# A graph layer on one core: six edges in a partition instead of eight, 36-node spans about each group's middle edge, a written instruction order

## The chip, the core and the metric

The kernel runs on one core of a Trainium2 chip. The metric is device time in microseconds (us) of one execution, as the median of several runs; lower is better. A profile is one more execution, recorded by the hardware profiler.

## The reference

12,500 nodes have 128 features each (`x`), and 412,500 edges have 48 (`edge_attr_48`). `dst` gives each edge's node and is sorted, so a node's edges lie together: 33 of them on average, one of which is the node's own loop.

```python
h = jnp.maximum(_layernorm(x, axis=-1), 0.0)
agg = jax.ops.segment_sum(edge_attr_48, dst, num_segments=12500)
u = graph_globals[zeros(12500)]          # one graph
t = jnp.concatenate([h, agg, u], axis=1) # 128 + 48 + 64
out = x + jax.nn.relu(t @ W1 + b1) @ W2 + b2   # 240 -> 256 -> 128
```

All numbers are 32-bit floats.

## The kernel before

**Sums over edges.** A chunk is 1024 edges (`CE`), laid out as 128 partitions with 8 edges each (`T`); there are 403 chunks, the last one partly filled. Four chunks (`CG`) make a group, and there are 101 groups (`NG`). `group` (L186) loads a group's edges (768 KB, `load_edges`, L170), builds one-hot rows on VectorE (L194: 32 edge slots times 48 nodes, `W`, equal or not equal to the edge's place in its chunk's span), and lets TensorE multiply edges by one-hots (L201: 32 matmuls with 48 moving columns, put by turns into PSUM rows 0 to 47 and 64 to 111). `add` (L212) reads the group's first node into a register of VectorE (L207) and adds the group's PSUM tile, 141 nodes wide, into `aggT` at that node (L214). `aggT` holds the sums of all nodes, transposed.

**The spans and their check.** The place of an edge is its node less the base of its chunk, and the base (`brow`, L141) is the node of the group's first edge, less 8, plus 31 for each chunk. `read_dst` (L242) reads `dst` for 128 chunks with one chunk in a partition, subtracts the bases (L249), transposes the result into `rel`, and takes each chunk's least and greatest place (L251, L252). The last chunk has too few edges, so `load_dst` (L220) fills its row with the last edges of `dst` once more (L229); a filled slot has zero features, so it changes no sum. L267 to L281 fold the extremes into one flag: `bad` (L279) becomes 1 if any place lies outside 0 to 47, or if the groups' first nodes run too far from an even pace. Every engine loads the flag into a register (L280), and if it is 1, the block from L284 to L333 runs.

**The block behind the flag.** It serves any input: it clears `aggT`, finds each chunk's least and greatest node, and then loops over the chunks at run time (L325), one chunk in a round. A round loads the chunk's edges into a single buffer, reads the two nodes into registers (L308), and runs an inner loop over windows of 64 nodes (L313): one-hots, eight matmuls, and one addition into `aggT`. At the end it sets `rel` so that the groups that follow add nothing. In the profile no line between L285 and L333 appears.

**The MLP.** Nodes go in 25 blocks: one of 212 and 24 of 512. `normalize` (L364) takes mean and variance on VectorE and scale and shift on ScalarE. `mlp` (L382) adds `b2` to `x` on GpSimd (L386), normalizes on ScalarE (L390), transposes on TensorE (L392), copies to SBUF on ScalarE (L395), multiplies by `W1` (L399 for `h`, L400 for the sums), applies relu on ScalarE (L402), multiplies by `W2` (L407), adds on VectorE (L409) and stores. A block may start when the groups that hold its nodes have been added (`ready`, L91).

**Order.** A scheduler of the language places the instructions on each engine; the program states only the order of the calls (L420 to L438). Edge loads and stores go through SP's DMA queue, `x` and the weights through ScalarE's.

Of the kernel before, what the change touches and what calls it, by code (L numbers as in the profile page):

```python
# [9 lines left out]
F32 = mybir.dt.float32  # L10
# [11 lines left out]
def kernel(  # L22
# [24 lines left out]

    nc = tc.nc
# [4 lines left out]
    T = 8  # L53
    CE = P * T
    CG = 4
    GE = CG * CE
    STEP = N * CE // E
    SL = 8
    W = 48
    WG = STEP * (CG - 1) + W  # L60
# [12 lines left out]
    EARLY = 6  # L73
    MARGIN = 64
    GSTEP = CG * STEP
# [13 lines left out]
    supers += [rest[i:i + XB] for i in range(0, len(rest), XB)]  # L89

    ready = [min(NG - 1, -(-(a + R * m + MARGIN) // GSTEP) - 1) for a, m in blocks]  # L91

    const = ctx.enter_context(tc.tile_pool(name="const", bufs=1))
    big = ctx.enter_context(tc.tile_pool(name="big", bufs=1))
    psum = ctx.enter_context(tc.tile_pool(name="ps_agg", bufs=1, space=bass.MemoryType.PSUM))

    rel = big.tile([P, NB * P, T], F32)
    aggT = big.tile([P, N + SL + WG], F32)
    brow = const.tile([1, NB * P], F32)
    lo_i = const.tile([1, NG], I32)  # L100
    span = const.tile([P, NB, 2], F32)
    bad = const.tile([1, 1], I32)

    first = const.tile([1, NG], I32)
    with nc.allow_non_contiguous_dma(reason="a hundred numbers, once"):
        nf = E // GE
        nc.sync.dma_start(first[:, :nf], dst[:nf * GE].rearrange("(a g e) -> a g e", a=1, e=GE)[:, :, 0])
        if nf < NG:
            nc.sync.dma_start(first[:, nf:NG], dst[None, nf * GE:nf * GE + 1])

    one = const.tile([1, 1], F32)
    nc.gpsimd.memset(one, 1.0)
    steps = const.tile([1, NG, CG], F32)
    nc.gpsimd.iota(steps, pattern=[[0, NG], [STEP, CG]], base=-SL, channel_multiplier=0,
                   allow_small_or_imprecise_dtypes=True)
    least = const.tile([1, NG], F32)
    nc.gpsimd.iota(least, pattern=[[GSTEP, NG]], base=-MARGIN, channel_multiplier=0,
                   allow_small_or_imprecise_dtypes=True)
    ident = const.tile([P, P], F32)
    make_identity(nc, ident)  # L120
    iota = const.tile([P, WA], F32)
    nc.gpsimd.iota(iota, pattern=[[1, WA]], base=0, channel_multiplier=0,
                   allow_small_or_imprecise_dtypes=True)
    eps = const.tile([P, 1], F32)
    nc.gpsimd.memset(eps, EPS)
    nc.gpsimd.memset(aggT, 0.0)
    nc.gpsimd.memset(span, 0.0)
    warm = const.tile([P, 1], F32)
    nc.scalar.activation(warm, eps, AF.Sqrt, bias=eps)

    acc = []
    for i in range(3):
        ps = psum.tile([P, 512], F32, name=f"ps{i}")
        nc.vector.memset(ps, 0.0)
        acc.append(ps)


    lo_f = const.tile([1, NG], F32)
    nc.vector.tensor_scalar(lo_f, first, 0.0, float(N - 1), OP.max, OP.min)
    nc.vector.tensor_copy(lo_i, lo_f)  # L140
    nc.vector.tensor_tensor(brow[:, :NG * CG].rearrange("a (g k) -> a g k", k=CG), steps,  # L141
                            lo_f[:, :, None].to_broadcast([1, NG, CG]), OP.add)


    w1h = const.tile([D, H], F32)
    w1a = const.tile([P, H], F32)
    w1u = const.tile([G, H], F32)
    w2 = const.tile([P, NH, D], F32)
    b1_sb = const.tile([P, NH], F32)
    u = const.tile([G, 1], F32)  # L150
    b2_sb = const.tile([P, D], F32)
    bias = const.tile([P, NH], F32)
    nc.gpsimd.memset(w1a, 0.0)

    def load_weights():
        nc.scalar.dma_start(w1h, W1[0:D])
        nc.scalar.dma_start(w1a[0:DE], W1[D:D + DE])
        nc.scalar.dma_start(w1a[HI:K2], W1[D:D + DE])
        nc.scalar.dma_start(w1u, W1[D + DE:D + DE + G])
        nc.scalar.dma_start(w2, W2.rearrange("(a p) d -> p a d", p=P))  # L160
        with nc.allow_non_contiguous_dma(reason="a few hundred numbers, once"):
            nc.scalar.dma_start(b1_sb, b1.rearrange("(a p) -> p a", p=P))
            nc.scalar.dma_start(u, graph_globals[0:1].rearrange("a g -> g a"))
        nc.scalar.dma_start(b2_sb, b2[None, :].to_broadcast([P, D]))

    ep = ctx.enter_context(tc.tile_pool(name="edges", bufs=8))
    ohp = ctx.enter_context(tc.tile_pool(name="oh", bufs=3))
# [18 lines left out]
    def group(g):  # L186
        c0 = g * CG
        n = min(CG, NCH - c0)
        wg = STEP * (n - 1) + W
        e = ep.tile([P, CG, T * DE], F32, name="e")  # L190
        load_edges(e, c0, n)
        oh = ohp.tile([P, CG * T, W], F32, name="oh")
        r = rel[:, c0:c0 + n, :].rearrange("p c t -> p (c t)")
        nc.vector.tensor_tensor(  # L194
            oh[:, :n * T], iota[:, None, :W].to_broadcast([P, n * T, W]),
            r[:, :, None].to_broadcast([P, n * T, W]), OP.is_equal)
        ps = acc[g % len(acc)]
        for k in range(n):
            for t in range(T):
                h = HI * (t % 2)  # L200
                nc.tensor.matmul(  # L201
                    ps[h:h + DE, STEP * k:STEP * k + W], e[:, k, t * DE:(t + 1) * DE], oh[:, k * T + t, :],
                    start=(k == 0 and t < 2), stop=(k == n - 1 and t >= T - 2), skip_group_check=True)
        return ps, wg

    def first_node(g):
        _, at = nc.values_load_multi_w_load_instructions(  # L207
            lo_i[0:1, g:g + 1], engines=[DVE], min_val=0, max_val=N - 1,
            skip_runtime_bounds_check_because="clamped to 0..N-1 on the chip")
        return at[0]  # L210

    def add(g, ps, wg):  # L212
        at = first_node(g)
        nc.vector.tensor_tensor(aggT[:K2, ds(at, wg)], aggT[:K2, ds(at, wg)], ps[:K2, :wg], OP.add)  # L214


    with tc.tile_pool(name="dst", bufs=2) as dp, tc.tile_pool(
        name="ps_dst", bufs=2, space=bass.MemoryType.PSUM
    ) as ps_dst:
        def load_dst(b):  # L220
            rows = min(P, NCH - b * P)
            full = min(P, NFULL - b * P)
            di = dp.tile([P, CE], I32, name="di")
            if full:
                nc.sync.dma_start(
                    di[:full], dst[b * P * CE:(b * P + full) * CE].rearrange("(c e) -> c e", e=CE))
            if full < rows:
                nc.sync.dma_start(di[full:rows, :TAIL], dst[None, E - TAIL:E])
                nc.sync.dma_start(di[full:rows, TAIL:], dst[None, E - (CE - TAIL):E])  # L229
            return di, rows  # L230

        def spread(b, df, rows):
            dv = df.rearrange("c (p t) -> c t p", t=T)
            for t0 in range(0, T, 4):
                pt = ps_dst.tile([P, 4, P], F32, name="ptd")
                for t in range(4):
                    nc.tensor.transpose(pt[:, t, :rows], dv[:rows, t0 + t, :], ident[:rows, :rows])
                nc.scalar.copy(  # L238
                    rel[:, b * P:b * P + rows, t0:t0 + 4].rearrange("p c t -> p t c"),
                    pt[:, :, :rows])  # L240

        def read_dst(b):  # L242
            di, rows = load_dst(b)
            df = dp.tile([P, CE], F32, name="df")
            pb = ps_dst.tile([P, 1], F32, name="pb", bufs=1)
            nc.tensor.matmul(pb[:rows], brow[:, b * P:b * P + rows], one, start=True, stop=True)  # L246
            base = dp.tile([P, 1], F32, name="base")
            nc.vector.tensor_copy(base[:rows], pb[:rows])
            nc.vector.tensor_scalar(df[:rows], di[:rows], base[:rows], None, OP.subtract)  # L249
            spread(b, df, rows)  # L250
            nc.vector.tensor_reduce(span[:rows, b, 0:1], df[:rows], AX.X, OP.min)  # L251
            nc.vector.tensor_reduce(span[:rows, b, 1:2], df[:rows], AX.X, OP.max)  # L252

        read_dst(0)
        load_weights()
        waiting = []
        for g in range(EARLY):
            waiting.append((g, *group(g)))
            if len(waiting) > 1:
                add(*waiting.pop(0))  # L260
            if g + 1 < NB:
                read_dst(g + 1)
        for w in waiting:
            add(*w)


        worst = const.tile([P, NB, 2], F32)  # L267
        nc.vector.tensor_scalar(worst[:, :, 0], span[:, :, 0], -1.0, None, OP.mult)
        nc.vector.tensor_scalar(worst[:, :, 1], span[:, :, 1], float(1 - W), None, OP.add)
        wcol = const.tile([P, 1], F32)  # L270
# [163 lines left out]
    for w in waiting:  # L434
        add(*w)
# [31 lines left out]
```

## Time and profile before

| | |
|---|---|
| median of 3 runs | 418.35 us (418.1 to 421.17) |
| the profiled execution, its own time | 418.65 us |
| its span, first to last instruction | 416.9 us |
| TensorE matmuls, busy | 342.9 us, 82% of the span |
| VectorE busy | 283.7 us, 68% |
| ScalarE, GpSimd busy | 106.4 us, 81.0 us |
| moved by DMA | 95.20 MB, 228 GB/s on average |
| first edge matmul starts at | 23.2 us |

The profiled execution took 0.3 us more than the median. Of its 418.65 us, 1.75 us lie outside the span. In the profile's rows PE is TensorE, PEld its weight loads, DVE VectorE, ACT ScalarE, POOL GpSimd and SP the engine that issues DMAs; a q behind the name means the engine's sequencer. A 32-bit matmul stands in the trace as two records. L201 is line 201 of the kernel.

### The profile page before, as it was taken

The page shows a single profiled execution, that of the slowest core. Times are in us where ns is not written, and L with a number is a line of the kernel's source. Part 1 is how long each engine was busy: PE and PEld are TensorE (multiplying, and loading weights), DVE is VectorE, ACT ScalarE, POOL GpSimd, SP SyncE. Part 2 cuts the span into 40 slices and gives each one's busy share as a digit, 9 for nine tenths or more (in the row PEclk, how much of TensorE's full clock was granted, in tenths as well). Part 3 has the DMA queues.
Part 4 walks back from the last instruction along what each step waited for, and adds up shares of the span by engine and source line. Part 5 has one row for each costly group of instructions (what it writes and reads, how often), then busy time and mean ns, then how long its engine had stood idle before and what let it go on. Part 6 is the DMA issues. An engine that isn't in the chain of part 4 may idle for free.

```text
span 416.9 us, 15948 instructions
## 1 busy us (share of the span) xinstructions
PE 342.9 (82%) x7193; PEld 270.0 (65%) x7194; DVE 283.7 (68%) x472; ACT 106.4 (26%) x193; POOL 81.0 (19%) x41
## 2 busy tenths in 40 slices
PE   0487569998699989898986997995979998888985
PEld 0377555785477677577565777774768776757853
DVE  7898598764965696786377788467675668629510
ACT  1140027312213303331230330330321332131231
POOL 9300021120221120222022022112022112203200
PEclk9995689999999999999899999999889999989999
DMA  5997693559847978877596697696583898654000
GB/s 163 323 370 264 207 346 126 188 197 308 286 141 239 323 255 304 281 248 233 179 322 217 225 316 233 192 342 219 198 302 109 257 325 270 194 198 156 29 13 39
DMA packets 61720, 95.20 MB, mean 228 GB/s; under 512 B 2760, under 2 KB 54996, under 8 KB 61649
## 3 DMA queue, kind: packets, MB, share of 16 engines
q1 hardware_dynamic: 57287, 87.26, 62.4%
q10 hardware_dynamic: 4362, 6.89, 4.7%
q8 instruction: 57, 0.93, 0.9%
q14 instruction: 14, 0.11, 0.1%
HBM read 87.74 MB, written 6.40 MB: 226 GB/s over the span
## 4 chain that ended last, share of the span: by engine, by line
PE 40%; issue 17%; DMA 10%; DVE 10%; POOL 5%; ACT 3%; DVEq 1%; ACTq 0%; POOLq 0%
PE ps L201 17%; DMA xt<-in_x_dram 10%; PE po L407 8%; PE ph L399 7%; PE ph L400 6%; POOL xb L386 5%; DVE oh L194 4%; DVE st L372 3%; ACT hT L395 3%; PE pt L392 2%; DVE mv L373 1%; DVE ot L409 1%; DVE aggT L214 1%; DVEq L207 1%; ACT hid L402 0%
## 5 line engine op out<-in xcount | busy, mean ns | idle before, releaser
L201 PE MATMUL ps<-oh,e 128*48 128x48 f32 x6448 | 175.8, 214 | 39.4 <-issue 17.7
L201 PEld LDWEIGHTS ps<-oh,e 128*48 128x48 f32 x6448 | 163.2, 130 | 53.8 <-DVE oh L194 21.9
L194 DVE TENSOR_TENSOR oh<-iota,rel 128x1536 f32<-128x1536 f32 (+1 forms) x101 | 194.0, 1936 | 2.3 <-ACT rel L238 1.3
L386 POOL TENSOR_TENSOR xb<-xt,b_sb 128x512 f32<-128x512 f32 (+1 forms) x25 | 67.7, 2709 | 313.6 <-DVE ot L409 273.6
L395 ACT COPY hT<-pt 128x512 f32<-128x512 f32 (+1 forms) x25 | 26.9, 1076 | 186.3 <-PE pt L392 186.3
L399 PE MATMUL ph<-hT,w1h 128*128 128x512 f32 (+1 forms) x100 | 56.4, 647 | 8.0 <-ACT hT L395 7.9
L214 DVE TENSOR_TENSOR aggT<-aggT,ps 112x141 f32 (+1 forms) x101 | 29.6, 293 | 47.8 <-PE ph L400 44.0
L407 PEld LDWEIGHTS po<-w,hid 128*128 128x128 f32 (+1 forms) x400 | 49.9, 189 | 16.5 <-issue 10.4
L407 PE MATMUL po<-w,hid 128*128 128x128 f32 (+1 forms) x400 | 55.4, 281 | 1.2 <-ACT hid L402 1.1
L409 DVE TENSOR_TENSOR ot<-po,xb 128x512 f32<-128x512 f32 (+1 forms) x25 | 17.2, 688 | 51.3 <-PE po L407 49.0
L400 PE MATMUL ph<-aggT,w1a 112*128 112x512 f32 (+1 forms) x100 | 52.0, 602 | 0.0
L402 ACT ACTIVATE hid<-ph,bias 128x512 f32<-128x512 f32 (+1 forms) x50 | 33.6, 676 | 47.5 <-PE ph L400 47.5
L390 ACT ACTIVATE xn<-xt,sh,sc 128x128 f32<-128x128 f32 (+1 forms) x100 | 40.7, 484 | 3.7 <-DVE sh L378 3.7
L372 DVE BATCH_NORM_STATS2 st<-xt 128x6 f32<-128x128 f32 (+1 forms) x100 | 25.1, 262 | 22.0 <-DMA xt<-in_x_dram 22.0
L400 PEld LDWEIGHTS ph<-aggT,w1a 112*128 112x128 f32 x100 | 20.3, 203 | 24.6 <-issue 24.0
L399 PEld LDWEIGHTS ph<-hT,w1h 128*128 128x128 f32 x100 | 18.3, 204 | 23.0 <-ACT hT L395 10.3
L392 PE MATMUL pt<-ident,xn 128*128 128x128 f32 (+1 forms) x100 | 18.1, 296 | 1.6 <-ACT xn L390 1.2
L373 DVE BATCH_NORM_AGGREGATE mv<-st 128x2 f32<-128x6 f32 (+1 forms) x100 | 15.6, 162 | 0.0
L246 PE MATMUL pb<-one,brow 1*128 1x1 f32 (+1 forms) x8 | 2.0, 312 | 14.6 <-DVE brow L141 13.8
L392 PEld LDWEIGHTS pt<-ident,xn 128*128 128x128 f32 (+1 forms) x100 | 11.1, 144 | 3.8 <-POOL xb L386 1.3
L376 ACT ACTIVATE sc<-mv,eps 128x16 f32<-128x16 f32 (+1 forms) x7 | 2.1, 305 | 42.0 <-DVE mv L373 42.0
L238 ACT COPY rel<-ptd 128x512 f32<-128x512 f32 (+1 forms) x8 | 6.7, 910 | 20.7 <-DMA w1a<-in_L_gnn_W_dram 13.4
(46 smaller groups left out, 59.9 us busy)
## 6 DMA issues: line engine op xcount, KB each, us to landing
e<-in_edge_attr_dram SPq DMA_DIRECT2D x100, 768.0 KB, 7.5
xt<-in_x_dram ACTq DMA_DIRECT2D x6, 1024.0 KB
out_dram<-ot SPq DMA_DIRECT2D x24, 256.0 KB, 5.3
di<-in_dst_dram SPq DMA_DIRECT2D x3, 512.0 KB, 11.1
e<-in_edge_attr_dram SPq DMA_DIRECT2D x1, 384.0 KB, 6.5
e<-in_edge_attr_dram SPq DMA_DIRECT2D x1, 159.0 KB
w1h<-in_L_gnn_W_dram ACTq DMA_DIRECT2D x1, 128.0 KB
w<-in_L_gnn_W_dram ACTq DMA_DIRECT2D x1, 128.0 KB, 4.2
```

The lines of the kernel that those rows point to most:

```text
L194: nc.vector.tensor_tensor(oh[:, :n * T], iota[:, None, :W].to_broadcast([P, n * T, W]), r[:, :, None].to_broadcast([P, n * T, W]), OP.is_e ...
L201: nc.tensor.matmul(ps[h:h + DE, STEP * k:STEP * k + W], e[:, k, t * DE:(t + 1) * DE], oh[:, k * T + t, :], start=(k == 0 and t < 2), stop= ...
L214: nc.vector.tensor_tensor(aggT[:K2, ds(at, wg)], aggT[:K2, ds(at, wg)], ps[:K2, :wg], OP.add)
L372: nc.vector.bn_stats(st[:m, i * R + r, :], xs[j][:m, r, :])
L386: nc.gpsimd.tensor_tensor(xb[:m], xs[j][:m], b2_sb[:m, None, :].to_broadcast([m, R, D]), OP.add)
L390: nc.scalar.activation(xn[:m, r], xs[j][:m, r], AF.Relu, bias=shift[j][:m, r:r + 1], scale=scale[j][:m, r:r + 1])
L392: nc.tensor.transpose(pt[:, r, :m], xn[:m, r], ident[:m, :m])
L395: nc.scalar.copy(hT[:, :n].rearrange("d (p r) -> d r p", r=R), pt[:, :, :m])
L399: nc.tensor.matmul(ph[:, :n], w1h[:, a * P:(a + 1) * P], hT[:, :n], start=True, stop=False)
L400: nc.tensor.matmul(ph[:, :n], w1a[:K2, a * P:(a + 1) * P], aggT[:K2, SL + a0:SL + a0 + n], start=False, stop=True)
L402: nc.scalar.activation(hid[:, a, :, :m], ph[:, :n].rearrange("h (p r) -> h r p", r=R), AF.Relu, bias=bias[:, a:a + 1])
L407: nc.tensor.matmul(po[:m, r], hid[:, a, r, :m], w2[:, a], start=(a == 0), stop=(a == NH - 1))
```

## The change

- A chunk is 768 edges, six in a partition; there are 538 chunks, and the last one holds 84 edges. Six chunks make a group (4608 edges, 36 one-hot slots, 864 KB), and there are 90 groups.
- A span is 36 nodes. The base of a chunk counts from the node of the group's middle edge (`mids`) with steps of 23 or 24 nodes (`OFF` is -76, -53, -29, -6, 17, 41). Places are now measured from the middle of the span, `MID` = 17.5, so that one reduction of the absolute value per 128 chunks replaces the two of before (`check_dst`), and the flag becomes 1 if the greatest absolute value is above 17.5 (`decide`).
- The row of the last chunk is filled as before: `load_dst` is the same text with the new sizes, so the fill is 684 edges.
- The block behind the flag stays, as the function `any_order`; its loop has 537 rounds and one more for the last chunk.
- `aggT` is cleared by ScalarE in five pieces (`clear`) and no longer by GpSimd (L126). The first eight groups' edges are issued at the start, and each later one behind a group's matmuls. `x` plus `b2` moves from GpSimd to VectorE. The variance comes from the halves that the statistics instruction gives, for 16 rows at once, in place of L373.
- `tc.manual_schedule()` makes each engine's order that of the calls. The MLP is cut into pieces (two `hidden`, one `transpose` of the next block, one `output`), which are dealt out between groups by a running budget; `store` follows one group later.

```diff
-    T = 8
+    T = 6
-    CG = 4
+    CG = 6
-    STEP = N * CE // E
-    SL = 8
-    W = 48
+    SL = 6
+    W = 36
+    MID = (W - 1) / 2
+    OFF = [round(N * CE / E * (k - CG / 2)) - SL for k in range(CG)]
...
+    ctx.enter_context(tc.manual_schedule())
...
-        nc.sync.dma_start(first[:, :nf], dst[:nf * GE].rearrange("(a g e) -> a g e", a=1, e=GE)[:, :, 0])
+    mids = [min(g * GE + GE // 2, E - 1) for g in range(NG)]
+        nc.sync.dma_start(first[:, :h], dst[:h * GE].rearrange("(a g e) -> a g e", a=1, e=GE)[:, :, GE // 2])
...
+    for k in range(CG):
+        nc.gpsimd.memset(steps[:, :, k], OFF[k] + MID)
...
+    nc.vector.tensor_scalar(iota, iota, -MID, None, OP.add)
...
-            nc.vector.tensor_reduce(span[:rows, b, 0:1], df[:rows], AX.X, OP.min)
-            nc.vector.tensor_reduce(span[:rows, b, 1:2], df[:rows], AX.X, OP.max)
+    def check_dst(b, df, rows):
+        nc.vector.tensor_reduce(span[:rows, b:b + 1], df[:rows], AX.X, OP.max, apply_absolute_value=True)
...
+    def decide():
+        wcol = const.tile([P, 1], F32)
+        nc.vector.tensor_reduce(wcol, span, AX.X, OP.max)
...
+        nc.vector.tensor_scalar(wrow[:, :P], pw, -MID, None, OP.add)
+        nc.vector.tensor_scalar(least, least, GSTEP, float(LEAST), OP.mult, OP.add)
+        nc.vector.tensor_tensor(wrow[:, P:], least, lo_f, OP.subtract)
+        wmax = const.tile([1, 1], F32)
+        nc.vector.tensor_reduce(wmax, wrow, AX.X, OP.max)
+        nc.vector.tensor_scalar(bad, wmax, 0.0, 1.0, OP.max, OP.min)
...
+    onehot(0)
+    for g in range(EARLY):
...
+        onehot(g + 1)
+        contract(g)
+        load_group(g + PF)
+        if g:
+            add(g - 1)
...
+    isbad = nc.values_load(bad[0:1, 0:1], min_val=0, max_val=1,
+                           skip_runtime_bounds_check_because="clamped to 0..1 on the chip")
+    any_order(isbad, hots[EARLY])
...
+    for g in range(EARLY, NG + LAG):
+        if g < NG:
+            onehot(g + 1)
+            contract(g)
+            load_group(g + PF)
+        if EARLY <= g - 1 < NG:
+            add(g - 1)
+        for j in late:
+            store(j)
...
+        while nextp < len(pieces) and done < budget and (pieces[nextp][1] <= g or g >= NG):
+            cost, _, run = pieces[nextp]
+            run()
```

`onehot`, `contract` and `add` hold what `group` and `add` held. The functions of the fill and of the block, as they stand in the changed kernel:

```python
    def load_dst(b):
        rows = min(P, NCH - b * P)
        full = min(P, NFULL - b * P)
        di = dp.tile([P, CE], I32, name="di", bufs=3)
...
        if full < rows:
            nc.sync.dma_start(di[full:rows, :TAIL], dst[None, E - TAIL:E])
            nc.sync.dma_start(di[full:rows, TAIL:], dst[None, E - (CE - TAIL):E])
...
                with tc.For_i(0, NFULL, 1) as c:
                    e = ap.tile([P, T * DE], F32, name="e2")
                    nc.sync.dma_start(e, edge_attr[ds(c * CE, CE)].rearrange("(p t) d -> p (t d)", t=T))
                    windows(e, rel[:, ds(c, 1), :].rearrange("p c t -> p (c t)"), ds(c, 1))
```

`windows` is the inner loop of before (L307 to L323) with six matmuls in place of eight.

## The prediction

> **What bounds the kernel now.** I read the engines' shares on the page first, then the page's groups, then the busy time of the edge matmuls in three stretches of the steady stage.
>
> ```profile
> PE 342.9 (82%) x7193; PEld 270.0 (65%) x7194; DVE 283.7 (68%) x472; ACT 106.4 (26%) x193; POOL 81.0 (19%) x41
> ```
>
> ```profile
> L201 PE MATMUL ps<-oh,e 128*48 128x48 f32 x6448 | 175.8, 214 | 39.4 <-issue 17.7
> L399 PE MATMUL ph<-hT,w1h 128*128 128x512 f32 (+1 forms) x100 | 56.4, 647 | 8.0 <-ACT hT L395 7.9
> L407 PE MATMUL po<-w,hid 128*128 128x128 f32 (+1 forms) x400 | 55.4, 281 | 1.2 <-ACT hid L402 1.1
> L400 PE MATMUL ph<-aggT,w1a 112*128 112x512 f32 (+1 forms) x100 | 52.0, 602 | 0.0
> ```
>
> ```profile
> 318.00:322.80 4.80, 4.80 (x210) 4.74 (x210) 1.00 0.56 151
> ```
>
> TensorE is the bound. Where it has work, 210 records of edge matmuls take 4.80 us (the columns are PE and PEld busy, with counts): 22.9 ns each, without a gap. From 318 to 400 us it is busy for 74.5 of 82 us. VectorE's largest group, the one-hots (101 times 1936 ns), runs beside it. So by its shares this is a kernel that could gain from narrower spans and fewer waits. What decides here, though, is a place of the profile that is nearly empty: the passage of the flag. These are the answers for the tile `bad` and for the branch at L284 (duration min/median/max in ns, then the first and last start in us), and then what followed in order of time (start and duration in us).
>
> ```profile
> L279 DVE TENSOR_SCALAR bad<-wmax x1: 142/142/142, 43.9 to 43.9; 1x1 int32<-1x1 f32 x1
> L280 PEldq TENSOR_LOAD <-bad x1: 488/488/488, 44.1 to 44.1; - x1
> ```
>
> ```profile
> L284 SPq EVENT_SEMAPHORE  x9: 17/17/17, 45.2 to 48.2; - x9
> ...
> L284 PEldq COMPARE_BRANCH  x1: 444/444/444, 44.7 to 44.7; - x1
> ```
>
> ```profile
> 45.71 0.52 PEld L344 LDWEIGHTS po<-u,w1u 64*128 64x128 f32 x4 [2.75 <-PEq L284]
> ...
> 48.34 0.32 ACTq L358 DMA_DIRECT2D xt<-in_x_dram  x1
> ```
>
> The flag is written at 44.09 us, every engine loads it and branches, and the next work is line 344, behind the block. The block was not entered. To pass it cost TensorE 1.6 us (45.71 - 44.09) and ScalarE 4.25 us (48.34 - 44.09).
>
> **Part 1: which way the flag falls.** The flag depends on `dst` alone, so it can be worked out by hand. The last chunk (537) is chunk 3 of group 89. That group's middle edge is 89 x 4608 + 2304 = 412,416, only 84 edges before the end; its node is 12,497. The middle of the chunk's span is 12,497 + OFF[3] + MID = 12,497 - 6 + 17.5 = 12,508.5. The chunk has 84 edges of its own, and its row in the check is filled with the last 684 edges of `dst`. At 33 edges to a node these reach back 20.7 nodes: to node 12,479. The place of that one is 12,479 - 12,508.5 = -29.5, and the limit is 17.5. So `decide` sees 29.5 - 17.5 = 12, clamps it to 1, and the flag is up. All other chunks lie within 15.5; the real edges of the last one do as well. A filled slot adds nothing to the sums, but the check counts it. Before, the fill was 172 edges, about five nodes, and all places lay from 4 to 46 in a span of 0 to 47; so the trace passed by. I therefore forecast that the changed kernel enters `any_order` on these inputs: the sums of the first groups are thrown away, all chunks are summed in a loop at run time, `rel` is overwritten, and the main loop then runs in full on one-hots that match nothing.
>
> **Part 2: one round of the loop.** No row of before shows it, so it is put together, with ends for each piece.
> - The edges' load. 144 KB go into a single buffer, and SP lets nobody into the inner loop until all its transfers are in. The issue of an edge load is 0.37 us in the timeline. The nearest rows for the landing:
>
> ```profile
> w1u<-in_L_gnn_W_dram ACTq DMA_DIRECT2D x1, 64.0 KB, 2.3
> w<-in_L_gnn_W_dram ACTq DMA_DIRECT2D x1, 128.0 KB, 4.2
> ```
>
>   Both stem from a start with full queues, and in the loop nothing else moves. I take 2.6 + 0.4 = 3.0 us (ends 2.3 and 4.6). The two register loads (0.3 to 0.5 us each) lie under it.
> - Three meetings of all five engines: into the inner loop, back out of it, and back to the next round. Each is drains, semaphores and a branch. The nearest row is the passage above: 1.6 us as TensorE saw it, of which 0.5 was the register's load, but that was one wait, and a loop's back edge has to reset semaphores between two of them. I take 1.5 us each, 4.5 in a round. [...] Ends: 0.7 us (the rows of single branches and semaphores are 17 to 444 ns) and 3.2.
> - The work between. Shift of the places 0.17 us; one-hot of 384 elements, from 1.72 us for 1536: 0.43, with a fixed part 0.5; twelve records of 64 columns, from 22.9 ns at 48: 12 x 30 ns = 0.37, with their latency 0.6; the addition 0.3, as L214; hand-overs 0.3. Together 1.9 us (1.3 to 2.2). A chunk's span is below 64 nodes, so the inner loop runs once.
>
> A round: 3.0 + 4.5 + 1.9 = 9.4 us (5.7 to 16.4). There are 537 rounds and the last chunk's: 538 x 9.4 = 5057 us. Nothing hides it: `add` on VectorE, the next groups' matmuls, the prefetched edges and the loads of `x` all stand behind the block on their engines and queues.
>
> **Part 3: around the loop.** GpSimd clears `aggT` (10.6 us in L126's row), five loads of `dst` of up to 384 KB (6.5 us each in the row of an edge load of that size, 32), `rel` is overwritten (3840 of 12,649 columns of 10.6: 3.2): 46 us.
>
> **Part 4: the rest of the change, which gives the frame.** The start: L139, an instruction over 101 numbers, took 9.4 us in the trace and ended with GpSimd's 10.6 us memset beside it; with that memset moved to ScalarE, the first edge matmul comes at about 14 us instead of 23.2 (an estimate: 23.2 less the 9). Edge matmuls: 3228, 6456 records. If a record goes with its columns, it takes 22.9 x 36/48 = 17.2 ns, in all 111 us. [...] The blocks: transposes 0.60, hidden 3.55, output 2.0 in the timeline around 330 us, 6.15 x 24.4 = 150 us, unchanged. Waits inside: 9% of TensorE's time in the steady stage, 27 us, though pieces dealt between groups should lower them. The tail: 12 us after the last edges as from 405 to 417, and about 2 outside the span. 14 + 148 + 150 + 27 + 12 + 2 = 353, say 355 us. Ends: 318 (with 111) and 395 (edge packets of 1152 instead of 1536 bytes at the same 73 ns each, that is queue 1's 62.4% of 16 x 416.9 us over 57,287 packets: 358 us of DMA at the fullest share seen, 0.92). VectorE gets `x` plus `b2` (25 x 0.7 us, by L409's row) and loses a quarter of each one-hot; it stays under TensorE.
>
> Sum: 355 + 46 + 5057 = 5458, say 5460 us. It is made against the profiled execution (418.65 us), 0.3 us from the median; at this size that is nothing.
>
> **The rivals.**
> 1. The flag stays down, and the kernel is faster: 355 us (318 to 395). The place is `check_dst`: the row's places run from -29.5 to -9.5, and if the absolute value is applied to the row's greatest value and not to its elements, 9.5 is seen instead of 29.5, which is under 17.5. One reduction decides over 5100 us. For it: no row of before shows a reduction with this option. [...] 13%.
> 2. The block is entered, and every meeting costs ScalarE's 4.25 us: 3.0 + 12.75 + 1.9 = 17.7 us a round, 9900 us. For it: the one ScalarE row. Against: TensorE's row. 4%.
> 3. The flag stays down and the change does nothing for TensorE and loses to DMA what the start gains: within 1% of before. Against: even the 395 above is 6% faster. 1%, within the 13.
>
> **How the numbers follow.** The block is entered: 87%, and 5460 us is its time. Rounds of 5.7 to 16.4 us give 3470 to 9220 us; I give 3450 to 9200. Rival 2 and what else lies outside take some 5%, so 82% are inside. Rival 1 would need a range from 318 us and is left out with its 13%. About 1% is what a measurement of this kernel can tell from no change. Faster 12%, within it 1%, slower 87%.
>
> **What would show it.** A profile of more than 3000 us, with lines 335 to 347 some 538 times each, TensorE busy for a tenth of the span, and the chain of waits made of branches and semaphores. Wrong: no line of the block in the profile; then Part 1 failed in how the absolute value is taken, and 355 is to be compared. If it is entered and the time is outside, the meetings (4.5 of 9.4 us) are the term to look at first.

## The result, and the profile after

The changed kernel takes 4111.86 us (4104.91 to 4116.76, four runs) against 419.76 us for the kernel before in the same session: a ratio of 9.79 (95% interval 9.73 to 9.85). The profiled execution has a span of 4109.0 us. Forecast were 5460 us, with a range of 3450 to 9200.

The engines' shares, the first rows of the 40 slices and the granted clock, from the page of the changed kernel:

```profile
PE 1156.0 (28%) x13697; PEld 969.8 (24%) x13698; DVE 842.0 (20%) x2592; ACT 114.1 (3%) x211; POOL 18.4 (0%) x25
...
PE   3222222222222222222222222222222222223998
...
PEclk6555555555555555555555555555555555555999
```

In these rows a digit is a tenth: from the second slice to the 37th TensorE is busy for some two tenths of the time and is granted half its clock (0.50 from 80 to 3780 us). The main loop stands in the last three slices. The block behind the flag is in the groups of the page (busy us, mean ns, then the idle time before them):

```profile
L344 PE MATMUL ps<-oh,e 128*48 128x64 f32 x6456 | 814.5, 316 | 2873.5 <-DVE oh L340 2873.5
...
L335 DVE TENSOR_SCALAR r<-rel 128x6 f32 x538 | 92.2, 171 | 1852.8 <-PEq L331 1848.4
L340 DVE TENSOR_TENSOR oh<-iota_a,r 128x384 f32<-128x384 f32 x538 | 300.2, 558 | 59.2
L347 DVE TENSOR_TENSOR aggT<-aggT,ps 48x64 f32 x538 | 115.2, 214 | 901.7 <-PE ps L344 901.7
L155 PE MATMUL ps<-oh,e 128*48 128x36 f32 x6456 | 165.5, 218 | 15.1 <-issue 11.7
```

Lines 335 to 347 stand there 538 times each: all edges were summed there, 537 chunks in the loop and the last one behind it. L155 has its full 6456 records as well, so the main loop ran too, over one-hots that match nothing. In order of time, one round of the loop and most of the next (start and duration in us; the row of SP's queue merges the issues of two rounds):

```profile
1999.95 0.17 DVE L335 TENSOR_SCALAR r<-rel 128x6 f32 x1 [3.43 <-PEq L331]
2000.64 0.17 DVE L338 TENSOR_SCALAR r<-r 128x6 f32<-128x6 f32 x1 [0.51 <-DVE r L335]
2000.92 0.56 DVE L340 TENSOR_TENSOR oh<-iota_a,r 128x384 f32<-128x384 f32 x1
...
2001.53 1.52 PE L344 MATMUL ps<-oh,e 128*48 128x64 f32 x12 [5.33 <-DVE oh L340]
2003.16 0.21 DVE L347 TENSOR_TENSOR aggT<-aggT,ps 48x64 f32 x1 [1.68 <-PE ps L344]
2005.77 7.22 SPq L351 DMA_DIRECT2D e<-in_edge_attr_dram  x2
2006.79 0.17 DVE L335 TENSOR_SCALAR r<-rel 128x6 f32 x1 [3.42 <-PEq L331]
2007.48 0.17 DVE L338 TENSOR_SCALAR r<-r 128x6 f32<-128x6 f32 x1 [0.51 <-DVE r L335]
...
2008.37 1.51 PE L344 MATMUL ps<-oh,e 128*48 128x64 f32 x12 [5.32 <-DVE oh L340]
```

A round takes 6.84 us here. It splits into 0.5 us between L335 and L338 (into the inner loop), 2.9 us of work from L338 to the end of L347, counting L335, and 3.4 us from there to the next L335 (out of the inner loop, back edge, two register loads).

The whole span: 61 us until GpSimd clears `aggT`, 31 us of preparation, 538 rounds of 6.86 us (3690), and 328 us for `rel` and the main loop behind it.

### The profile page after: what moved, and what is told of

The parts are those of the page before. It is cut to its first block, busy times and chain, and to the rows that moved or that the text cites. A ratio compares the mean times of both kernels' runs of the same rounds, so it can differ in the third digit from the quotient of the medians.

```text
span 4109.0 us, 113807 instructions
## 1 busy us (share of the span) xinstructions
PE 1156.0 (28%) x13697; PEld 969.8 (24%) x13698; DVE 842.0 (20%) x2592; ACT 114.1 (3%) x211; POOL 18.4 (0%) x25
## 5 line engine op out<-in xcount | busy, mean ns | idle before, releaser
L344 PE MATMUL ps<-oh,e 128*48 128x64 f32 x6456 | 814.5, 316 | 2873.5 <-DVE oh L340 2873.5
L344 PEld LDWEIGHTS ps<-oh,e 128*48 128x48 f32 x6456 | 699.2, 198 | 2988.7 <-DVE oh L340 2983.4
L335 DVE TENSOR_SCALAR r<-rel 128x6 f32 x538 | 92.2, 171 | 1852.8 <-PEq L331 1848.4
L340 DVE TENSOR_TENSOR oh<-iota_a,r 128x384 f32<-128x384 f32 x538 | 300.2, 558 | 59.2
L347 DVE TENSOR_TENSOR aggT<-aggT,ps 48x64 f32 x538 | 115.2, 214 | 901.7 <-PE ps L344 901.7
L155 PE MATMUL ps<-oh,e 128*48 128x36 f32 x6456 | 165.5, 218 | 15.1 <-issue 11.7
L155 PEld LDWEIGHTS ps<-oh,e 128*48 128x48 f32 x6456 | 158.9, 130 | 30.6 <-issue 22.9
L338 DVE TENSOR_SCALAR r<-r 128x6 f32<-128x6 f32 x538 | 92.2, 171 | 275.3 <-DVE r L335 275.3
L145 DVE TENSOR_TENSOR oh<-iota,rel 128x1296 f32<-128x1296 f32 x90 | 134.5, 1494 | 0.6 <-ACT rel L190 0.6
L165 DVE TENSOR_TENSOR aggT<-aggT,ps 112x153 f32 x90 | 27.7, 308 | 87.8 <-PE ph L470 69.2
L189 PE MATMUL ptd<-ident,df 128*128 128x128 f32 (+1 forms) x60 | 14.1, 401 | 27.0 <-DVE df L198 21.0
```

The lines of the kernel that those rows point to most:

```text
L145: nc.vector.tensor_tensor(oh[:, :n], iota[:, None, :].to_broadcast([P, n, W]), r[:, :, None].to_broadcast([P, n, W]), OP.is_equal)
L155: nc.tensor.matmul(ps[h:h + DE, o:o + W], e[:, k, t * DE:(t + 1) * DE], oh[:, k * T + t, :], start=(k == 0 and t < 2), stop=(k == n - 1 an ...
L335: nc.vector.tensor_scalar(r, r_view, float(WA), None, OP.add)
L338: nc.vector.tensor_scalar(r, r, float(-WA), None, OP.add)
L340: nc.vector.tensor_tensor(oh, iota_a[:, None, :].to_broadcast([P, T, WA]), r[:, :, None].to_broadcast([P, T, WA]), OP.is_equal)
L344: nc.tensor.matmul(ps, e_view[:, t * DE:(t + 1) * DE], oh[:, t, :], start=(t == 0), stop=(t == T - 1))
```

## The experiments

My theory: the filled slots of the last chunk's row raise the flag, and the rounds of the block are the price. Rivals: something else raises it, or the written order and the new sizes are dear by themselves.

**The row filled with its own edges.**

```diff
-            nc.sync.dma_start(di[full:rows, TAIL:], dst[None, E - (CE - TAIL):E])
+            q = CE // TAIL
+            nc.sync.dma_start(di[full:rows, TAIL:q * TAIL].rearrange("a (r e) -> a r e", e=TAIL),
+                              dst[None, None, E - TAIL:E].to_broadcast([1, q - 1, TAIL]))
+            if q * TAIL < CE:
+                nc.sync.dma_start(di[full:rows, q * TAIL:], dst[None, E - (CE - q * TAIL):E])
```

> The changed kernel with one edit: the free slots of the last chunk's row in the check are filled with the chunk's own 84 edges over and over, and no longer with the last 684 edges; their places are then -11.5 to -9.5, inside the limit of 17.5. My theory, that the filled slots alone raise the flag: the block is passed by and no line of it is in the profile. The time is then what stands around the block in the changed kernel's trace, 57 us before it, 328 us behind it, some 2 us to pass, 2 outside the span: about 389 us, where the prediction's frame had 355 (318 to 395). The rival, that the flag is raised by something else (the groups' pace, or real edges outside the narrower span): 4110 us, unchanged.

Measured: 403.62 us (399.86 to 405.09) against 423.5 for the kernel before, ratio 0.958 (0.950 to 0.967). No line of the block is in the profile. One row of fill was worth 3700 us, and neither the groups' pace nor a real edge raises the flag. Without it the rest of the change gains 4%, and not the 15% of the prediction's frame.

**The limit moved around 29.5.**

```diff
-        nc.vector.tensor_scalar(wrow[:, :P], pw, -MID, None, OP.add)
+        nc.vector.tensor_scalar(wrow[:, :P], pw, -28.5, None, OP.add)
```

> The changed kernel with the old fill and the limit of the check set to 28.5 in place of 17.5. My theory says that the greatest absolute place is 29.5, so the flag stays at 1 and the time at 4110 us. If the absolute value were taken in another way, or if some place between 17.5 and 28.5 had raised the flag, it falls: about 389 us.

The second run has -29.5 in that place.

> As the run before, with the limit set to 29.5. My theory: 29.5 - 29.5 = 0, the flag is 0 and the block is passed by, about 389 us. If a place beyond -29.5 exists, or the flag comes from the groups' pace, 4110 us.

Measured, one run each: 4106.83 us and 400.03 us. With the old fill in both, a shift of the limit by one node turns the block on and off where the hand calculation put the filled slot. It also shows that the absolute value is taken of the row's elements: of its greatest value (-9.5) it would have been 9.5, below either limit.

**The kernel before, with its flag held up.**

```diff
-        nc.vector.tensor_scalar(bad, wmax, 0.0, 1.0, OP.max, OP.min)
+        nc.vector.tensor_scalar(bad, wmax, 1.0, 1.0, OP.max, OP.min)
```

> The kernel before with its flag held at 1, nothing else changed. If the price lies in the block alone, which both kernels have, its 403 rounds cost what a round of the changed kernel costs (6.86 us in its trace) plus four more matmul records at 127 ns and 128 more one-hot elements, about 7.5 us: 403 x 7.5 + 45 + 418 = 3490 us. The rival, that the block of before was cheap and the changed sizes or the written order make it dear: under 1500 us.

Measured, one run: 3380.66 us. Two starts of its rounds in order of time:

```profile
1000.73 0.17 DVE L312 TENSOR_SCALAR r<-rel 128x8 f32 x1 [2.50 <-PEq L325]
...
1007.98 0.17 DVE L312 TENSOR_SCALAR r<-rel 128x8 f32 x1 [2.45 <-PEq L325]
```

7.25 us a round, 403 rounds: 2922 us on top of 418; the other 40 us are the block's clearing and preparation. The block was as dear before; it was only never entered. The changed kernel's is dearer in all because smaller chunks make a third more rounds.

**One round taken apart: without the inner loop, and without the load.**

```diff
-                    with tc.For_i(lo, hi + 1, WA) as at:
-                        at = nc.s_assert_within(at, 0, N - 1, skip_runtime_bounds_check_because="at most hi")
+                    at = nc.s_assert_within(lo, 0, N - 1, skip_runtime_bounds_check_because="the only window")
```

The loop's body moves out by one level with it.

> The changed kernel, with the inner loop over windows taken out of the block: its body runs once in a round, in a straight line (on these inputs the inner loop ran once as well). Two of the three meetings of a round are gone. By the prediction's term (1.5 us a meeting) a round falls by 3.0 us, to 3.9, and the kernel to about 2500 us. By its lower end (0.7 us), which the round of 6.86 us in the trace suggests, it falls by 1.4 us, to 5.5, and the kernel to about 3360 us. If the edges' load comes to the path in their place, less is saved: 3500 us and more.

In the second kernel every round but the last chunk's multiplies the edges of the first chunk:

```diff
+                e = ap.tile([P, T * DE], F32, name="e2")
+                nc.sync.dma_start(e, edge_attr[0:CE].rearrange("(p t) d -> p (t d)", t=T))
                 with tc.For_i(0, NFULL, 1) as c:
-                    e = ap.tile([P, T * DE], F32, name="e2")
-                    nc.sync.dma_start(e, edge_attr[ds(c * CE, CE)].rearrange("(p t) d -> p (t d)", t=T))
```

> The changed kernel with the edges of one chunk loaded once ahead of the loop, and no load in its rounds; it leaves out the loads, so the sums are of other edges. By the prediction's term the load lies on the path and a round loses up to 2.5 us (0.4 of issue, 2.1 to the landing): about 2770 us. By the trace the matmuls start 2.6 us after the load's issue in any case, behind the register loads, the entry of the inner loop and the one-hot: then the load is hidden, and the time stays within 5% of 4110 us.

Measured, one run each: 3334.38 us without the inner loop, 4105.65 us without the load. The second lies within the four runs of the changed kernel (4104.91 to 4116.76), so the load cost nothing that can be seen. Its line in the changed kernel, and then the straight round in order of time:

```profile
L351 SPq DMA_DIRECT2D e<-in_edge_attr_dram x537: 332/336/381, 77.3 to 3769.2; - x179
...
DMA to landing us min/median/max: 1.9/2.1/2.2
```

```profile
1001.92 0.56 DVE L339 TENSOR_TENSOR oh<-iota_a,r 128x384 f32<-128x384 f32 x1
...
1003.05 1.49 PE L343 MATMUL ps<-oh,e 128*48 128x64 f32 x12 [3.95 <-DMA e<-in_edge_attr_dram]
```

With the inner loop, the matmuls start 2.6 us after the load's issue in any case (2005.77 to 2008.37), and the data are there 2.1 us after it. In the straight round the one-hot ends at 1002.48, and TensorE waits another 0.57 us, now for the load. So taking out two meetings won 1.45 us a round ((4112 - 3334) / 538) although 0.57 us of load came out from behind them: together 2.0, an estimate of about 1.0 us for each meeting.

**Spans of 48 nodes again.**

```diff
-    SL = 6
-    W = 36
+    SL = 12
+    W = 48
```

> The kernel with the refilled row, and its spans set back to 48 nodes about the same middles (the flag stays down). If a matmul record of the edges is at a floor that does not depend on its columns, as the prediction took it, TensorE's work is the same and the time stays within 1% of that of the refilled kernel, about 400 us; VectorE's one-hots grow by 90 x 0.45 = 40 us beside it. If records go with their columns, 6456 x 5.7 ns = 37 us come on top: 437 us.

Measured: 405.88 us, ratio to the kernel before 0.962 (0.952 to 0.973), beside 0.958 (0.950 to 0.967) with 36. From the chains of waits (start, duration, work) of the kernel with 36 columns, and of the one with 48:

```profile
349.15 5.11 PE ps L155 x221
...
362.52 4.99 PE ps L155 x216
```

```profile
353.43 5.12 PE ps L155 x221
...
366.72 5.11 PE ps L155 x216
```

That is 23.1 ns a record in both stretches with 36 columns, and 23.2 and 23.7 ns with 48. A quarter of the columns is worth next to nothing, and the two times cannot be told apart.

**Another start.** The loads of all `dst` rows ahead of the second group's edges, the weights and the first `x` ahead of ScalarE's copies, the first large `x` before the flag, six groups ahead:

```diff
-    PF = 8
+    PF = 6
...
-    dis = {0: load_dst(0)}
+    dis = {0: load_dst(0), 1: load_dst(1)}
     load_group(0)
-    dis[1] = load_dst(1)
+    load_weights()
+    for b in range(2, NB):
+        dis[b] = load_dst(b)
     load_group(1)
-    dis[2] = load_dst(2)
+    load_x(0)
     for g in range(2, PF):
         load_group(g)
...
+        if g == 3:
+            load_x(1)
```

> The kernel with the refilled row and another start: all node indices are loaded ahead of the second group of edges, the weights and the first block of x are issued before ScalarE's copies, the first large load of x comes before the flag's passage, and six groups of edges are kept ahead in place of eight. In the refilled kernel's trace TensorE is idle for 37 of the 78 us from 12 to 90 us, against 17 of 295 after that. If these waits are the 45 us by which the refilled kernel missed the predicted frame of 355 us, most of them go: 365 to 380 us. If the start is held by what the DMA engines can move, or if fewer groups ahead cost later what is won here, it stays at 395 to 405 us.

Measured: 384.86 us (382.25 to 387.09), ratio 0.914 (0.906 to 0.922). It beats both kernels. PE and PEld busy in three stretches, of the refilled kernel first, then of this one (the other engines, clock and DMA behind them):

```profile
12.00:60.00 48.00, 24.41 (x536) 22.27 (x534) 18.07 (x29) 14.86 (x12) 0.00 (x0) 0.89 0.68 225
60.00:90.00 30.00, 16.12 (x255) 12.45 (x256) 14.49 (x44) 7.59 (x19) 0.00 (x0) 0.77 0.66 222
90.00:150.00 60.00, 58.72 (x1359) 45.92 (x1358) 39.35 (x67) 17.25 (x35) 0.00 (x0) 1.00 0.89 283
```

```profile
12.00:60.00 48.00, 31.13 (x669) 28.13 (x671) 28.07 (x68) 19.01 (x21) 0.00 (x0) 0.79 0.91 315
60.00:90.00 30.00, 29.89 (x617) 22.66 (x614) 19.39 (x25) 11.32 (x25) 0.00 (x0) 1.00 0.77 244
90.00:150.00 60.00, 58.01 (x1291) 44.67 (x1289) 39.06 (x85) 18.35 (x37) 0.00 (x0) 1.00 0.90 291
```

Of 37.5 idle us of TensorE between 12 and 90, 17.0 are left, all before 60; the DMA engines' share of that stretch rose from 0.68 to 0.91, which may leave little room there for earlier loads. By the medians the gain is 19 us, short of the 20 to 35 us expected; the two profiled executions are only 13.5 us apart (spans of 398.1 and 384.6), for with 20.5 idle us less, TensorE's work between the start and the tail took 4.6 us more, and the idle time behind 90 us and the tail took 2.4 us more.

## Why the prediction was right, and where its sums were off

**Part 1, the flag.** Right, and settled by the three runs on fill and limit. The chance of 13% went to an absolute value taken of the result; the limit runs exclude it here. Of the signs named, the lines of the block came 538 times each; the chain of waits cannot be read, because it reaches back only to 4042.83 us, far behind the loop.

**Part 2, a round: 9.4 us forecast, 6.86 measured.** The picture of a round was right, meetings and then a chain of work with nothing beside them; the load on its path was not, and the terms were off in both directions. The measured round lies near the lower end of a wide range (5.7 to 16.4).
- The load: 3.0 us forecast, nothing measured. The step that failed is "SP lets nobody into the inner loop until all its transfers are in". VectorE's first instruction in the inner loop starts at 2007.48, 0.5 us after L335, and the load issued at 2005.77 lands 2.1 us later, at 2007.87; only the matmuls wait for the data, and by then they are there. The 2.1 us count from the start of the issue (0.34 us), so they stand against 3.0 forecast.
- The meetings: 4.5 us forecast, 3.9 measured, with VectorE's two register loads (0.31 us each), which were put under the load and, by the wait before L335 (<-PEq L331, the line of these loads), lie on the path. A meeting is worth about 1.0 us, by the estimate above, and not 1.5; the 3.2 us at the upper end of that term stand on no row. At the outer loop's line (L349) each engine drains twice a round, SP three times, and has three to five semaphore instructions; at the inner loop's line (L336) each has eight of these and three branches, and no drain. Rival 2, with 4.25 us at every meeting, would have made 12.75 us. It did not come. The larger of the two queues that the page calls instruction moved as much in the changed kernel (first row) as in the kernel before, so the rounds loaded nothing more through it:

```profile
q8 instruction: 57, 0.93, 0.1%
```

```profile
q8 instruction: 57, 0.93, 0.9%
```

  What ScalarE's 4.25 us went to stays open: the row of L284 in the prediction has SP at its semaphores until 48.2 us, just before ScalarE goes on at 48.34, so it may have waited for SP.
- The work: 1.9 us forecast, 2.9 measured. Twelve records took 1.52 us and not 0.6: 127 ns each, where 30 were taken. They were priced at the full clock of the steady stage (1.00 from 318 to 322.8 us in the kernel before), and in the loop TensorE is granted half of it (0.50). That is only part of the reason. The rows show the loop's records, and then the main loop's just behind the block, both at a clock of 0.50 (us, PE and PEld busy, clock):

```profile
2001.50:2003.10 1.60, 1.52 (x12) 1.30 (x12) 0.50 0.00 0
```

```profile
3780.90:3784.10 3.20, 3.10 (x72) 2.97 (x72) 0.50 0.20 61
```

  A record of 36 columns takes 43 ns there, against 23.1 at a clock of 1.00 (221 records in 5.11 us from 4060.37 us on). For 64 columns that makes 77 ns in proportion, an estimate, and not 127 (some 110 without the end of the last record, by the page's mean of 316 ns for one). What adds the rest was not taken apart. One difference is in the code: the main loop's matmuls go by turns into two sets of PSUM rows, the block's all into one. The longer records and the shorter span are also why "TensorE busy for a tenth of the span" came out as 28%.

0 + 3.9 + 2.9 = 6.8. The missing 2.5 us times 538 are 1370 us. The distance between 5460 and 4112 is 1348; Part 3 took 12 us too much, and the frame of Part 4 some 30 too little.

**Part 3.** 46 us forecast; 31 for the preparation and 3.3 for `rel` measured.

**Part 4, the frame of 355 us: measured 404.** One judgement held: edge records gain nothing from 36 columns. The sum's 148 us are 6456 records at the 22.9 ns that a record of 48 columns took; that 36 columns take as long was not shown by any run before the prediction. The runs show 23.1 ns with 36 columns, and 23.2 and 23.7 with 48. The upper end of 395 us had no ground, though the measured time exceeds it: it charged 73 ns for each of the smaller packets. Queue 1 of the refilled kernel,

```profile
q1 hardware_dynamic: 74452, 87.26, 66.5%
```

gives 66.5% of 16 x 398.1 us over 74,452 packets: 57 ns each.

Two terms failed, which the refilled kernel's profiled execution shows: its span of 398.1 us is 12 us of start, 318 of TensorE's work and 55 of its idle time between 12 and 385 us, and a tail of 13. The sum had 14, 298, 27 and 12.

The first is the price of the work, 20 us too low, some 15 of them for edge records. It was read off a stretch of 4.8 us without a gap. The same stage of the kernel before, from 318 to 400 us, has 1580 edge records in 40.39 us, 25.6 ns each (first row; PE busy with its count behind the comma). In the refilled kernel a record took 33.6 ns before 90 us, at a mean clock of 0.85, and 24.4 after it:

```profile
318.00:400.00 82.00, 40.39 (x1580) 37.90 (x1580) 0.98 0.58 192
```

```profile
12.00:90.00 78.00, 24.19 (x720) 23.14 (x720) 0.85 0.68 223
90.00:385.00 295.00, 138.77 (x5688) 133.17 (x5688) 0.98 0.77 251
```

The second is "Waits inside: 9% of TensorE's time in the steady stage, 27 us", taken for the whole run. (7.5 idle us of 82 are 9% of the stage, but 10% of the work in it; on 298 us of work that is 30.) The steady stage is better than that: 17 idle us of the 295 from 90 to 385. The waits between the first edge matmul and the steady stage, 37.5 us, are not in the sum at all. The first edge matmul did come early, at 12.2 us in the changed kernel (14 forecast), but then this was waited for, from the refilled kernel's waits (total us, times, longest):

```profile
ACT rel L194 <- PE ptd L193: 20.8, 3, 9.7
...
PE ptd L193 <- DVE df L202: 20.4, 4, 10.5
...
DVE st L427 <- DMA e<-in_edge_attr_dram: 12.3, 1, 12.3
...
DVE df L202 <- DMA di<-in_dst_dram: 10.3, 2, 6.8
ACT rel L194 <- DMA b_sb<-in_L_gnn_b_dram: 9.8, 1, 9.8
```

In this written order an engine stood at the first thing that was late, up to 12.3 us in one wait of these rows. The transposes of the next `dst` rows stand ahead of a group's matmuls on TensorE, those rows stand behind up to eight groups of edges in SP's queue, and ScalarE's copies stand behind its own weight loads. What this cost was shown in part: the last run, which moves these loads (and keeps six groups ahead), wins 19 us back. Which of the moves does it was not taken apart. Of the 34 us by which its span still exceeds the sum (351 without the 2 us outside), 25 are work priced too low (323 us between 12 and 370) and 8 are idle time (35 in place of 27; 17 of the 35 lie before 60 us).

## What to carry to other kernels

A flag that sends a kernel to a slow general path is part of its time: before anything is summed, work out its value on the given inputs, padding included, because padding that is harmless for the result need not be harmless for a check. A round of this run-time loop (6.86 us) cost its meetings of all engines (3.9 us) and a chain of work at half the clock (2.9 us at 0.50), and the load beside them was free until meetings were removed (then TensorE waited 0.57 us for it). Price work from a whole stage, and not from its best stretch. In a written order, look at the start first: what each engine will stand still for, and which queue that stands in.

## What was not expected of the hardware

- VectorE's first instruction over some hundred numbers took 9.39 us in the kernel before, beside GpSimd's memset of `aggT`, and 0.20 us in the changed one, where ScalarE clears it:

```profile
3.59 0.20 DVE L243 TENSOR_SCALAR lo_f<-first 1x90 f32<-1x90 int32 x1 [3.47 <-DMA first<-in_dst_dram]
```

  It came back in the block: the first cast of `dst` took 5.04 us beside GpSimd's memset there, and the later ones of that size about 0.54. No run changes the memset alone.

```profile
60.58 10.69 POOL L312 MEMSET aggT<- 128x12704 f32 x1 [3.02 <-DVE aggT L165]
...
66.63 5.04 DVE L317 CAST df<-di 128x768 f32<-128x768 int32 x1 [6.18 <-DMA di<-in_dst_dram]
...
75.24 0.54 DVE L317 CAST df<-di 128x768 f32<-128x768 int32 x1
```

- TensorE, busy for two tenths of its time (820 of 3700 us), was granted 0.50 of its clock for 3700 us on end (80 to 3780).
- To pass the flag when it is down took longer in the written order: from the flag's writing at 56.06 us to ScalarE's first load of `x` at 66.45 are 10.4 us in the refilled kernel, against 4.25 in the kernel before. Some of it is waiting for an engine with work ahead of the flag: in the changed kernel, where the flag is written at 56.6 us, ScalarE reads it at 56.7 and SP, behind its edge loads, at 60.5. The rest is not explained.
